# Routing the first sequence during layer A's last chunks, with tile pools split into groups

## The chip, the cores and the metric

The kernel runs on one core of one Trainium2 chip. The metric is the device time of one execution in microseconds (us). The time before is the median of three runs.

## What is computed

The reference works on two sequences of 1024 tokens with 512 features, in float32. Four layers follow one another, each a residual on a normalised input:

```python
x = x + attn_a(layernorm(x))      # layer A: Mamba2 chunked scan, 64 heads of 16, chunks of 128 tokens
x = x + ffn(layernorm(x))         # mixture of 8 experts, 2 per token, and shared experts
x = x + attn_b(layernorm(x))      # attention among the 16 heads of each token
x = x + ffn(layernorm(x))         # the same mixture again

def attn_a(u):
    xBCzA = u @ in_proj_w.T                       # x, B, C | z | A_log
    xBC = silu(causal_conv4(xBC))
    dt = softplus(A_log)
    # per chunk and head: Y_diag = (C B^T * exp(segsum(-dt))) X, Y_off from the carried state
    return ((y_ssm + D * x / dt) * silu(z + z_bias)) @ out_proj_w.T

def ffn(x):
    gates = softmax(x @ router_w.T)               # 8 experts
    masked = top2(gates) / (sum + 1e-20)
    routed = sum_e (silu(x @ wg[e]) * (x @ wu[e])) @ wd[e] * masked[:, e]
    return routed + (silu(x @ sg) * (x @ su)) @ sd      # the shared experts, 2 x 352 wide
```

`attn_b` has low-rank projections (Wc, Wcq, Wqr, Wckv, Wck, Wkr, Wv, Wo), a rotary part, and attention among the 16 heads of each token. It is not touched by the change; only the loads of its weights matter here.

## The kernel before

The residual `x` stays in SBUF as 16 tiles `xs` of 128 tokens, eight for each sequence. Line numbers are those of the kernel before.

**Layer A (L176 to L545)** works on 16 chunks of 128 tokens, two to a segment, first those of one sequence, then those of the other. For a segment, `segment_inputs` (L200) makes the projections on TensorE (`ps_ch` L285, `ps_z` L310), the convolution on VectorE (`chan` L288 to L292) and softplus, and writes the running sums of dt to DRAM (`sums`). For a chunk, `prologue` (L341) makes the chunk's x and B tiles, the carried state and `y`; `scores` (L421) makes `g`; `own` (L435) does the heads. `own` handles eight lots of eight heads, in two halves `e`. For each lot a tile `m` (128 x 8 x 128) is filled by a broadcasting DMA from `sums` (L449, on SyncE's queue, SP), then GpSimd subtracts (L453), ScalarE takes Relu and Exp (L455, L456), VectorE multiplies by `g` (L457), and TensorE adds 16 products to `ps_y` (L461). After a half, VectorE makes `yT` (L480); after both, `ps_out` (L487) is the projection back, and VectorE adds it to `x` (L495). The tag `m` has a ring of 8 buffers. The main loop calls `own` for one chunk after another as a generator; `due` and `rate` say after which of its steps a step of the next segment's inputs is taken, so that TensorE has both kinds of work in its queue. The order of instructions on each engine is the order in which these generators issue them, moved a little by a scheduler; each engine works through its own queue in order.

**The mixture (L586 to L873)** is a class `Mixture`, one object for each sequence and layer. `normalise(t)` (L709) has three steps for a tile of 128 tokens: normalise it and store its rows (`normed`, L712); transpose it (`ps_xnT`, L169; copied by ScalarE to `p_xnT`, L170) and store it (`columns`, L716); make the router's logits (`ps_p` L720, `parts` L722 on ScalarE, `ps_l` L724, `logits` L725). `route` (L586) has four steps and turns the logits of a sequence into a list of 23 blocks of 128 token slots: `r_e` (L617) marks the chosen experts, `ps_n` (L622 to L626) counts them, `ps_t` (L687) inverts the list, `r_tok` holds the tokens and `r_expi` the expert of each block. `units(lead)` (L766) is the main work: 16 shared units (two groups of shared experts by eight tiles) and 23 routed ones (the blocks), in an order that begins with `lead` shared units. Shared units read columns `xT` (L763) and weights `s_gu` and `s_d` (L742, on SP); routed ones read the block's expert number into a register on SP (L748), load that expert's `w_gu` and `w_d` (L742) and gather the tokens' rows `xg` with an indirect DMA of GpSimd (L753). A unit is `ps_g` (L816), Silu (L818), `ps_u` (L825), the product `h` (L826), three transposes `ps_hT` (L837), copies `hT` (L839, L840) and `ps_o` (L847). `after` (L856) gathers the routed results and adds them.

**The border between the two.** Layer A's pools (`a_w`, `a_seg`, `a_chunk`, `a_ps`) are closed after its last chunk, and the pools behind (`b_w`, `b_ffn`, `b_attn`, `b_ps`) are opened in the same memory: a tile of these waits for what lay there before. Just after the pools are opened, `w_router`, the attention's weights and biases are loaded in 18 DMAs from ScalarE's queue (L559, L567, L582). `w_router` and `quarters` serve `normalise`. Then the stages follow, where `run` (L1014) issues a step of its other arguments beside each step of the first, by a rate:

```python
first = [Mixture(b) for b in range(NB)]
for _ in each(first[0]):                     # all eight tiles of normalise, nothing beside them
    pass
run(first[0].units(5), 1.0, first[0].route(), each(first[1]), first[1].route())
second = [Mixture(b) for b in range(NB)]
run(first[1].units(0), 1.3, first[0].after(False), attention(0, second[0]))
run(second[0].units(6), 1.3, in_turn(first[1].after(False), second[0].route()), attention(1, second[1]))
run(second[1].units(6), 2.0, in_turn(second[0].after(True), second[1].route()))
```

Of the kernel before, what the change touches and what calls it, by code (L numbers as in the profile page):

```python
# [73 lines left out]

@with_exitstack
def hybrid_layer_kernel(ctx: ExitStack, tc: tile.TileContext, a: dict, out: bass.AP):
# [41 lines left out]
    def count(shape, pattern, base, channel_multiplier, name):  # L118

        whole = const.tile(shape, I32, name=name + "_i")  # L120
        nc.gpsimd.iota(whole, pattern=pattern, base=base, channel_multiplier=channel_multiplier)
        c = const.tile(shape, F32, name=name)
        nc.vector.tensor_copy(c, whole)
        return c

    token_of = count([P, TPB], [[P, TPB]], 0, 1, "token_of")
    place = count([P, P], [[1, P]], -P, 0, "place")
    block_of = count([P, NBLK], [[1, NBLK]], 0, 0, "block_of")
    block_at = count([P, NBLK], [[P, NBLK]], 0, 0, "block_at")
    minus_half = const.tile([P, 1], F32, name="minus_half")  # L130
# [41 lines left out]

    with ExitStack() as sa:
        wp = sa.enter_context(tc.tile_pool(name="a_w", bufs=1))  # L176
        sp = sa.enter_context(tc.tile_pool(name="a_seg", bufs=2))
        cp = sa.enter_context(tc.tile_pool(name="a_chunk", bufs=2))
        pp = sa.enter_context(tc.tile_pool(name="a_ps", bufs=2, space=PSUM))
# [20 lines left out]
        def segment_inputs(b, s, before):  # L200
# [32 lines left out]
            sv = sp.tile([P, n], F32, tag="sp_s", name="sp_s", bufs=1)  # L233
# [3 lines left out]
            acc = sp.tile([P, n], F32, tag="sp_acc", name="sp_acc", bufs=1)  # L237
# [197 lines left out]
        def own(c, gs, between):  # L435
# [8 lines left out]
            for e in range(2):  # L444
                ps = pp.tile([P, 4, P], F32, tag="y", name="ps_y", bufs=1)
                for i in range(4):
                    h0 = (2 * i + e) * 8
                    m = cp.tile([P, 8, P], F32, tag="m", name="m", bufs=8)
# [59 lines left out]

        for _ in inputs(0):
            pass  # L510
# [23 lines left out]
        for c in range(CHUNKS):  # L534
            steps = own(c, gs, before_chunk(c + 1))
            while True:
                try:
                    next(steps)
                except StopIteration as end:
                    gs = end.value  # L540
                    break
                due += rate
                while due >= 1.0:
                    due -= 1.0
                    next(side, None)  # L545

# [4 lines left out]
    fp = ctx.enter_context(tc.tile_pool(name="b_ffn", bufs=2))  # L551
    ap = ctx.enter_context(tc.tile_pool(name="b_attn", bufs=2))
    pp = ctx.enter_context(tc.tile_pool(name="b_ps", bufs=2, space=PSUM))
    dram = ctx.enter_context(tc.tile_pool(name="b_dram", bufs=4, space=bass.MemoryType.DRAM))


    w_router = wp.tile([P, KD, 32], F32, name="w_router")
    nc.vector.memset(w_router, 0.0)
    nc.scalar.dma_start(out=w_router[:, :, 0:NE], in_=a["routerT"].rearrange("(k p) e -> p k e", p=P))  # L559
    quarters = wp.tile([P, NE], F32, name="quarters")  # L560
    nc.vector.tensor_copy(quarters, ident[:, 0:NE])
    for k in range(1, KD):
        nc.vector.tensor_add(quarters, quarters, ident[:, 32 * k : 32 * k + NE])
# [21 lines left out]

    def route(logits):  # L586

        s3 = [P, TPB, NE]
        mx = fp.tile([P, TPB], F32, tag="r_mx", name="r_mx", bufs=1)
        nc.vector.tensor_reduce(mx, logits, AX.X, ALU.max)
        gt = fp.tile(s3, F32, tag="r_g", name="r_g", bufs=1)
        nc.vector.tensor_tensor(gt, logits, bc(mx, 2, NE), ALU.subtract)
        nc.scalar.activation(gt, gt, AF.Exp)
        sm = fp.tile([P, TPB], F32, tag="r_sm", name="r_sm", bufs=1)
        nc.vector.tensor_reduce(sm, gt, AX.X, ALU.add)
        nc.vector.reciprocal(sm, sm)  # L600
        nc.vector.tensor_tensor(gt, gt, bc(sm, 2, NE), ALU.mult)
        mine, other = bc(gt, 3, NE), bc(gt, 2, NE)
        n = TOPK * TPB
        ahead = fp.tile([P, TPB, NE, NE], F32, tag="r_room", name="r_ahead")
        more = fp.tile([P, TPB, NE, NE], F32, tag="r_room", name="r_more")
        nc.vector.tensor_tensor(ahead, other, mine, ALU.is_equal)
        nc.vector.tensor_tensor(ahead, ahead, bc(earlier, 1, TPB), ALU.mult)
        nc.vector.tensor_tensor(more, other, mine, ALU.is_gt)
        nc.vector.tensor_add(ahead, ahead, more)
        rank = fp.tile(s3, F32, tag="r_k", name="r_k", bufs=1)  # L610
        nc.vector.tensor_reduce(rank, ahead, AX.X, ALU.add)

        chosen = fp.tile([P, TOPK] + s3[1:], F32, tag="r_c", name="r_c", bufs=1)
        for c in range(TOPK):
            nc.vector.tensor_scalar(chosen[:, c], rank, float(c), None, ALU.is_equal)
        either = fp.tile(s3, F32, tag="r_e", name="r_e", bufs=1)
        nc.vector.tensor_add(either, chosen[:, 0], chosen[:, 1])  # L617
        yield


        ps_n = pp.tile([P, TPB + 1, NE], F32, tag="at", name="ps_n")
        nc.tensor.matmul(ps_n[:, 0:TPB], upper, either, start=True, stop=False)  # L622
        for t in range(1, TPB):
            nc.tensor.matmul(ps_n[:, t:TPB], ones, either[:, 0 : TPB - t], start=False, stop=(t == TPB - 1))
        for t in range(TPB):
            nc.tensor.matmul(ps_n[:, TPB], ones, either[:, t], start=(t == 0), stop=(t == TPB - 1))  # L626

        nc.vector.tensor_mul(gt, gt, either)
        nc.vector.tensor_reduce(sm, gt, AX.X, ALU.add)
        nc.vector.tensor_scalar(sm, sm, GATE_EPS, None, ALU.add)  # L630
        nc.vector.reciprocal(sm, sm)
        nc.vector.tensor_tensor(gt, gt, bc(sm, 2, NE), ALU.mult)
        picked = fp.tile([P, TOPK] + s3[1:], F32, tag="r_p", name="r_p", bufs=1)
        gates = fp.tile([P, TOPK, TPB], F32, tag="r_gates", name="r_gates")
        for c in range(TOPK):
            nc.vector.tensor_mul(picked[:, c], chosen[:, c], gt)
        nc.vector.tensor_reduce(gates, picked, AX.X, ALU.add)

        yield


        full = fp.tile([P, NE, TPB], F32, tag="r_e", name="r_full", bufs=1)
        nc.vector.tensor_tensor(full, bc(ps_n[:, TPB], 2, TPB), bc(block_at[:, 0:TPB], 1, NE), ALU.is_gt)
        blocks = fp.tile([P, NE], F32, tag="r_blocks", name="r_blocks", bufs=1)
        nc.vector.tensor_reduce(blocks, full, AX.X, ALU.add)
        before = fp.tile([P, NE, NE], F32, tag="r_k", name="r_before", bufs=1)
        nc.vector.tensor_tensor(before, earlier, bc(blocks, 1, NE), ALU.mult)
        first = fp.tile([P, NE], F32, tag="r_first", name="r_first", bufs=1)
        nc.vector.tensor_reduce(first, before, AX.X, ALU.add)
        past = fp.tile([P, NBLK, NE - 1], F32, tag="r_room", name="r_past")  # L650
        nc.vector.tensor_tensor(past, bc(block_of, 2, NE - 1), bc(first[:, 1:NE], 1, NBLK), ALU.is_ge)
        experts = fp.tile([P, NBLK], F32, tag="r_exp", name="r_exp", bufs=1)
        nc.vector.tensor_reduce(experts, past, AX.X, ALU.add)
        experts_i = fp.tile([P, NBLK], I32, tag="r_expi", name="r_expi")
        nc.vector.tensor_copy(experts_i, experts)


        nc.vector.tensor_scalar(first, first, float(P), -1.0, ALU.mult, ALU.add)
        number = fp.tile(s3, F32, tag="r_num", name="r_num", bufs=1)
        nc.vector.tensor_tensor(number, ps_n[:, 0:TPB], bc(first, 1, TPB), ALU.add)  # L660
        for c in range(TOPK):
            nc.vector.tensor_mul(picked[:, c], chosen[:, c], number)
        slot = fp.tile([P, TOPK, TPB], F32, tag="r_slot", name="r_slot", bufs=1)
        nc.vector.tensor_reduce(slot, picked, AX.X, ALU.add)
        slots = fp.tile([P, TOPK, TPB], I32, tag="r_slots", name="r_slots")
        nc.vector.tensor_copy(slots, slot)
        yield


        flat = slot.rearrange("p c t -> p (c t)")  # L670
        reached = fp.tile([P, n, NBLK], F32, tag="r_room", name="r_reached")
        nc.vector.tensor_tensor(reached, bc(flat, 2, NBLK), bc(block_at, 1, n), ALU.is_ge)
        block = fp.tile([P, n], F32, tag="r_blk", name="r_blk", bufs=1)
        nc.vector.tensor_reduce(block, reached, AX.X, ALU.add)
        offset = fp.tile([P, n], F32, tag="r_off", name="r_off", bufs=1)
        nc.vector.scalar_tensor_tensor(offset, block, float(-P), flat, ALU.mult, ALU.add)
        nc.vector.tensor_scalar(block, block, -1.0, None, ALU.add)
        nc.vector.tensor_tensor(reached, bc(block_of, 1, n), bc(block, 2, NBLK), ALU.is_equal)
        for c in range(TOPK):
# [12 lines left out]
        yield  # L692
        return gates, slots, tokens, experts_i

    class Mixture:

# [394 lines left out]
```

## Time and profile before

| what | value |
|---|---|
| median of 3 runs | 2448.04 us (2441.32 to 2453.75) |
| the profiled execution, its own time | 2449.53 us |
| its span in the profile | 2447.3 us, 29948 instructions |
| mean granted clock of TensorE | 0.964 |
| TensorE (PE) busy | 2254.1 us |
| VectorE (DVE) busy | 1401.5 us |
| GpSimd (POOL) busy | 1101.6 us |
| ScalarE (ACT) busy | 856.1 us |
| layer A | to 780.0 us, the end of its last `ps_out` |
| first mixture stage (`first[0].units`) | to 1161.85 us |

How the profile is read: one execution was recorded, and times are us from the start of its span. PE is TensorE's matmuls and PEld its weight loads, which lie beside them. "ACTq" and "SPq" are the issues of DMAs on the queues of ScalarE and SyncE; they are not counted as busy time of the engine. In a timeline a row has start, duration, engine, line, operation, and the tile written and those read, and behind them in brackets the idle time of that engine just before, with what ended it. PEclk is the clock that TensorE was granted, as a share of full speed.

### The profile page before, as it was taken

Reading aid. Unit: us, or ns where it says so; the run is one execution under the profiler, and the core shown is the slowest. Engines: PE = TensorE matmul, PEld = TensorE weight load, DVE = VectorE, ACT = ScalarE, POOL = GpSimd, SP = SyncE. Lnnn points to the kernel's source line nnn. Section 1 sums busy time; section 2 is a strip of 40 time slices with the busy share of each in tenths; the row PEclk is TensorE's granted clock in tenths of the full one; section 3 lists DMA queues with packets and bytes.
Section 4 is the critical chain, followed back from the end, with each engine's and each line's share of the span. In section 5 each row is a group of like instructions: output and inputs, shape, how many; then the busy total and the mean of one; then the engine's idle time right before and its main releaser. Section 6 shows DMA issues by size and latency. Waiting matters only on the chain.

```text
span 2447.3 us, 29948 instructions
## 1 busy us (share of the span) xinstructions
PE 2254.1 (92%) x10996; PEld 1450.8 (59%) x10996; DVE 1401.5 (57%) x2113; ACT 856.1 (35%) x1412; POOL 1101.6 (45%) x757
## 2 busy tenths in 40 slices
PE   7989999999996899999789899999988999899997
PEld 6766676676673556655555555556555555566564
DVE  6867777767764421002159888883688999620002
ACT  4665665666473331211122222221222323112221
POOL 3444553554463110002287777732878885210002
PEclk9999999999998899999899999999999999999998
DMA  8445454444444477775634454343555554468774
GB/s 278 150 137 169 136 172 157 157 164 148 154 167 153 160 250 248 297 263 202 220 128 162 168 191 161 135 144 108 212 186 188 182 186 149 159 252 298 263 267 139
DMA packets 119313, 456.42 MB, mean 187 GB/s; under 512 B 17280, under 2 KB 20096, under 8 KB 106368
## 3 DMA queue, kind: packets, MB, share of 16 engines
q1 hardware_dynamic: 86416, 384.87, 45.2%
q0 software_dynamic: 12480, 40.90, 5.5%
q10 hardware_dynamic: 20272, 28.74, 3.2%
q8 instruction: 88, 1.44, 0.2%
q14 instruction: 57, 0.47, 0.1%
HBM read 408.84 MB, written 45.61 MB: 186 GB/s over the span
## 4 chain that ended last, share of the span: by engine, by line
PE 59%; DVE 14%; POOL 9%; DMA 8%; ACT 6%; issue 4%; ACTq 0%; SPq 0%; POOLq 0%; DVEq 0%
PE ps_o L847 12%; PE ps_u L825 11%; PE ps_g L816 10%; PE ps_ch L285 6%; POOL pr L940 5%; PE ps_out L487 4%; DMA part<-made,r_slots 4%; DVE sc L941 3%; PE ps_z L310 3%; PE ps_xnT L169 2%; DMA m<-sums 2%; PE ps_y L461 2%; DVE o L958 2%; DVE pv L957 2%; PE ps_hT L837 2%
## 5 line engine op out<-in xcount | busy, mean ns | idle before, releaser
L940 POOL TENSOR_TENSOR pr<-qk 128x1536 f32<-128x1536 f32 x128 | 441.2, 3458 | 96.7 <-DVE sc L941 83.1
L453 POOL TENSOR_TENSOR m<-m,cum 128x1024 f32<-128x1024 f32 x128 | 241.7, 1897 | 338.6 <-DMA m<-sums 170.5
L826 DVE TENSOR_TENSOR h<-h,ps_u 128x352 f32<-128x352 f32 x156 | 80.5, 516 | 461.6 <-PE ps_u L825 457.4
L753 POOL DMA_INDIRECT xg<-normed,r_tok x92 | 90.2, 981 | 509.7 <-PE ps_xnT L169 438.2
L285 PE MATMUL ps_ch<-xnT,w_ch 128*128 128x259 f32 x1024 | 259.3, 402 | 15.6 <-DVE chan L292 14.8
L847 PE MATMUL ps_o<-w_d,hT 128*128 128x512 f32 x552 | 260.1, 603 | 0.2
L941 DVE TENSOR_REDUCE sc<-pr 128x32 f32<-128x1536 f32 x128 | 224.5, 1754 | 52.3 <-POOL pr L940 50.8
L818 ACT ACTIVATE h<-ps_g 128x352 f32<-128x352 f32 x156 | 72.3, 464 | 511.8 <-PE ps_g L816 505.3
L825 PE MATMUL ps_u<-w_gu,xT 128*128 128x352 f32 x736 | 242.0, 468 | 0.0
L816 PE MATMUL ps_g<-w_gu,xT 128*128 128x352 f32 x736 | 240.2, 465 | 0.9 <-DMA w_gu<-in_wall 0.8
L285 PEld LDWEIGHTS ps_ch<-xnT,w_ch 128*128 128x128 f32 x1024 | 194.2, 196 | 63.8 <-issue 32.6
L455 ACT ACTIVATE m<-m 128x1024 f32<-128x1024 f32 x128 | 134.2, 1053 | 195.1 <-POOL m L453 194.7
L847 PE MATMUL ps_o<-s_d,hT 128*128 128x512 f32 (+1 forms) x384 | 188.3, 621 | 8.2 <-ACT hT L839 6.2
L816 PEld LDWEIGHTS ps_g<-w_gu,xT 128*128 128x128 f32 x736 | 138.8, 192 | 95.6 <-issue 39.3
L853 ACT COPY y<-ps_o 128x512 f32<-128x512 f32 x92 | 53.9, 586 | 361.9 <-PE ps_o L847 361.9
L292 DVE SCALAR_TENSOR_TENSOR chan<-ps_ch,convw,chan 128x256 f32<-128x256 f32 x384 | 176.0, 476 | 4.7
L816 PE MATMUL ps_g<-s_gu,xT 128*128 128x352 f32 x512 | 171.3, 472 | 3.3 <-ACT h L818 1.9
L825 PEld LDWEIGHTS ps_u<-w_gu,xT 128*128 128x128 f32 x736 | 135.8, 195 | 64.4 <-issue 11.3
L825 PE MATMUL ps_u<-s_gu,xT 128*128 128x352 f32 x512 | 169.6, 467 | 0.0
L847 PEld LDWEIGHTS ps_o<-w_d,hT 128*128 128x128 f32 x552 | 105.2, 194 | 103.3 <-issue 85.6
L957 DVE TENSOR_TENSOR pv<-sc,vT 128x1024 f32<-128x1024 f32 x128 | 155.9, 1218 | 0.8
L958 DVE TENSOR_REDUCE o<-pv 128x64 f32<-128x1024 f32 x128 | 155.1, 1211 | 1.0
(209 smaller groups left out, 3532.0 us busy)
## 6 DMA issues: line engine op xcount, KB each, us to landing
w_gu<-in_wall SPq DMA_DIRECT2D x92, 1408.0 KB, 7.8
w_d<-in_wall SPq DMA_DIRECT2D x92, 768.0 KB, 4.6
m<-sums SPq DMA_DIRECT2D x128, 512.0 KB, 4.6
w_ch<-in_wch SPq DMA_DIRECT2D x96, 512.0 KB, 4.1
made<-y ACTq DMA_DIRECT2D x92, 256.0 KB, 6.6
xT<-columns SPq DMA_DIRECT2D x64, 256.0 KB, 4.8
s_gu<-in_wall SPq DMA_DIRECT2D x8, 1408.0 KB, 7.0
normed<-xn SPq DMA_DIRECT2D x32, 256.0 KB, 2.0
```

Of the source, the lines that this page charges most:

```text
L285: nc.tensor.matmul(ps, w[:, ct % 2, k], xnT[:, k, :], start=(k == 0), stop=(k == KD - 1))
L292: nc.vector.scalar_tensor_tensor(c[:, i], ps[:, tap : tap + SEG], convw[:, ct, tap : tap + 1], c[:, i], ALU.mult, ALU.add)
L453: nc.gpsimd.tensor_tensor(m, m, bc(cum[:, j, h0 : h0 + 8], 2, P), ALU.subtract)
L455: nc.scalar.activation(m, m, AF.Relu)
L487: nc.tensor.matmul(ps_out, yT[:, e, i, :], w_out[:, 2 * i + e, :], start=(e == 0 and i == 0), stop=(e == 1 and i == 3),)
L816: nc.tensor.matmul(ps_g, xT[:, k, :], both[:, k, 0, :], start=(k == 0), stop=(k == KD - 1))
L825: nc.tensor.matmul(ps_u, xT[:, k, :], both[:, k, 1, :], start=(k == 0), stop=(k == KD - 1))
L847: nc.tensor.matmul(ps_o, hT[:hn, c, :], wd[:hn, c, :], start=(c == 0), stop=(c == len(HC) - 1))
L940: nc.gpsimd.tensor_mul(pr, bc(qks[t][:, 0, i : i + IC, :], 2, AH), bc(qks[t][:, 1], 1, IC))
L941: nc.vector.tensor_reduce(scores[t][:, i : i + IC, :], pr, AX.X, ALU.add)
L957: nc.vector.tensor_tensor(pv, bc(scores[t][:, i : i + IC, :], 2, DH), bc(vs[t], 1, IC), ALU.mult)
L958: nc.vector.tensor_reduce(outs[t][:, i : i + IC, :], pv, AX.X, ALU.add)
```

## The change

- `route` and `Mixture` are defined ahead of layer A, with pools of their own (`mix`, `mix_dram`), which live to the end. `w_router` and `quarters` are made at the kernel's start. Their small PSUM tiles come from a helper `small`, in layer A under the tag `misc`, which `ps_out` uses too, later under `at`.
- The eight `normalise` of the first sequence and its `route` are issued as single steps during layer A's chunks of the second sequence, one step at every second step of `own`.
- `route` copies `ps_n` to a tile `counts`, and reads that.
- Four pools are split into groups (class `Pools`): `a_seg` in three, `a_ps` in four, `b_ffn` in four and `b_ps` in six, so that the memory of each comes free by itself. The integer tables of the start have a pool that is closed early. In softplus two tiles take the memory of others (`sv = y`, `acc = r`).
- The ring of `m` has 6 buffers, not 8.
- The first stage begins with 4 shared units, not 5, has no `normalise` and no `route` of its own sequence beside it, and loads `s_gu` and `s_d` of its first group from ScalarE's queue.

```diff
+class Pools:
+    def __init__(self, ctx, tc, name, groups, **kw):
+        self.pool_of = {}
+        for i, tags in enumerate(groups):
+            pool = ctx.enter_context(tc.tile_pool(name=f"{name}{i}", bufs=2, **kw))
+            self.pool_of.update((tag, pool) for tag in tags)
+    def tile(self, shape, dtype, tag, **kw):
+        return self.pool_of[tag].tile(shape, dtype, tag=tag, **kw)
...
+    mp = ctx.enter_context(tc.tile_pool(name="mix", bufs=2))
+    mdram = ctx.enter_context(tc.tile_pool(name="mix_dram", bufs=4, space=bass.MemoryType.DRAM))
+    small_tag = "misc"
+    def small(shape, name):
+        return pp.tile(shape, F32, tag=small_tag, name=name, bufs=2)
...
-        sp = sa.enter_context(tc.tile_pool(name="a_seg", bufs=2))
+        sp = Pools(sa, tc, "a_seg", [
+                ["xnT", "w_ch", "al", "sp_y", "sp_r", "sp_s2", "row"],
+                ["dt", "dw", "decay", "chan"],
+                ["cum", "gate0", "gate1"]])
-        pp = sa.enter_context(tc.tile_pool(name="a_ps", bufs=2, space=PSUM))
+        pp = Pools(sa, tc, "a_ps", [["y"], ["g0", "g1"], ["misc"], ["proj"]], space=PSUM)
...
-            sv = sp.tile([P, n], F32, tag="sp_s", name="sp_s", bufs=1)
+            sv = y
...
-            acc = sp.tile([P, n], F32, tag="sp_acc", name="sp_acc", bufs=1)
+            acc = r
...
-                    m = cp.tile([P, 8, P], F32, tag="m", name="m", bufs=8)
+                    m = cp.tile([P, 8, P], F32, tag="m", name="m", bufs=6)
...
+        first = [Mixture(b) for b in range(NB)]
+        routes = chain(*(first[0].normalise(t) for t in range(TPB)), first[0].route())
+        turn = 0
...
                 while due >= 1.0:
                     due -= 1.0
                     next(side, None)
+                if c >= TPB:
+                    turn += 1
+                    if turn % 2 == 0:
+                        next(routes, None)
+        for _ in routes:
+            pass
...
-    fp = ctx.enter_context(tc.tile_pool(name="b_ffn", bufs=2))
+    fp = Pools(ctx, tc, "b_ffn", [["s_gu", "s_d"], ["xT", "h", "hT"], ["w_gu"], ["w_d", "xg", "y", "part"]])
-    pp = ctx.enter_context(tc.tile_pool(name="b_ps", bufs=2, space=PSUM))
+    pp = Pools(ctx, tc, "b_ps", [["sc"], ["at"], ["o"], ["tr"], ["g"], ["u"]], space=PSUM)
+    small_tag = "at"
...
+        counts = mp.tile([P, TPB + 1, NE], F32, tag="r_n", name="r_n", bufs=1)
+        nc.vector.tensor_copy(counts, ps_n)
...
-        def weights(self, row):
+        def weights(self, row, queue=None):
...
-                nc.sync.dma_start(out=w, in_=src)
+                (queue or nc.sync).dma_start(out=w, in_=src)
...
-        def units(self, lead):
+        def units(self, lead, queue=None):
...
-            shared = {0: self.weights(NE)}
+            shared = {0: self.weights(NE, queue)}
...
-    first = [Mixture(b) for b in range(NB)]
-    for _ in each(first[0]):
-        pass
-    run(first[0].units(5), 1.0, first[0].route(), each(first[1]), first[1].route())
+    run(first[0].units(4, nc.scalar), 1.0, each(first[1]), first[1].route())
```

## The prediction

> **What bounds the kernel now.** I read the page first, part 1 and then its strips by slices (part 2), for the engine that is short and the places where it is not busy; then the chain of waits, the table by stage, the timeline of the worst stretch, and the instruction orders of both kernels.
>
> ```profile
> PE 2254.1 (92%) x10996; PEld 1450.8 (59%) x10996; DVE 1401.5 (57%) x2113; ACT 856.1 (35%) x1412; POOL 1101.6 (45%) x757
> PE   7989999999996899999789899999988999899997
> PEclk9999999999998899999899999999999999999998
> ```
>
> TensorE (PE) is busy 92% of the span, so a change pays by filling a hole. The hole is in slices 12 and 13 (one is 61.2 us): PE reads 6 and 8, the clock 8 and 8. That is the border between layer A (the chunks) and the mixtures. The table by stage (start and end, length, PE, PEld, VectorE, ScalarE and GpSimd busy, clock, DMA share, GB/s) cuts it out:
>
> ```profile
> 380.00:740.00 360.00, 344.64 (x2588) 249.72 (x2590) 259.83 (x441) 227.54 (x254) 184.59 (x119) 0.98 0.49 159
> 740.00:780.00 40.00, 30.84 (x336) 20.21 (x324) 18.42 (x20) 18.71 (x20) 19.23 (x11) 0.91 0.30 106
> 780.00:806.84 26.84, 5.04 (x33) 3.50 (x34) 3.34 (x12) 3.23 (x6) 2.11 (x6) 0.60 0.88 295
> 806.84:880.00 73.16, 69.57 (x358) 43.41 (x356) 26.88 (x81) 26.38 (x54) 16.08 (x35) 0.91 0.51 177
> 880.00:1162.00 282.00, 276.75 (x1023) 166.61 (x1021) 44.68 (x104) 61.60 (x157) 35.71 (x41) 0.98 0.71 252
> ```
>
> In the third row, from the last `ps_out` to the first unit's `ps_g`, PE is busy 5.04 of 26.84 us. The timeline (start, duration, engine) says why:
>
> ```profile
> 780.03 0.41 ACTq L567 DMA_DIRECT2D w_c<-in_Wc  x1
> ...
> 782.59 4.13 ACTq L567 DMA_DIRECT2D w_cq<-in_Wcq  x1
> ...
> 797.38 0.59 ACTq L567 DMA_DIRECT2D sin<-in_sin  x1
> 798.07 0.59 ACT L170 COPY p_xnT<-ps_xnT 128x512 f32<-128x512 f32 x1 [31.63 <-DMA b_rows<-in_brope]
> 798.71 0.65 PE L720 MATMUL ps_p<-p_xnT,w_router 128*32 128x128 f32 x8 [17.27 <-ACT p_xnT L170]
> ```
>
> Eighteen loads, w_router's and seventeen of attention weights, are issued from ScalarE's queue, and ScalarE computes nothing from 780.0 to 798.07. The copy that turns the first normalised tile stands behind them, and PE waits 17.27 us for it. The rest of the stretch is the serial `normalise` of the first sequence.
>
> **Why the parts move as they do.** In the new order the seventeen loads still stand after the last `ps_out` (`w_c` waits for PE, since the b_w tiles lie over layer A's memory). New is what lies around them. Ahead of the last `ps_out` stand `ps_g` and `ps_u` of unit 0, `ps_g` of unit 1 and half its `ps_u`, and one tile's transposes; behind it, before PE needs ScalarE again: the rest of `ps_u`, two `ps_hT`, `ps_g` and `ps_u` of unit 2, one `ps_p`. Then PE meets `ps_l`, which needs ScalarE's `parts` copy, and that is behind the loads.
>
> **Before, from 806.84 on.** The chain gives a steady unit as `ps_g` 2.37, `ps_hT` 0.33, transposes of a gathered tile 0.44, `ps_u` 2.37, `ps_o` 2.58 us: 8.09 routed, 7.65 shared. The 23 routed and 16 shared units make 308.5. Beside them run the rest of the first sequence's normalise (5.3), its route (0.17 + 1.52 + 1.79 and four lots of `ps_t`, 6.8), the second's normalise (8 × 0.97 = 7.8) and route (6.9): 335.3 in all. Losses: PE at half clock after idle times 1.3 + 1.7 + 2.7 + 1.7 = 7.4; the first gather, behind the late route, 3.6; the stage's last wait and the clock after it 5.1 + 2.6. 806.84 + 335.3 + 18.7 = 1160.8; the trace has 1161.85.
>
> **After, from the last `ps_out`.** Let E be what layer A becomes longer, so that `ps_out` ends at 780.0 + E. ScalarE is blocked for 18.0 and then copies `parts` (0.3): 798.3 + E. PE's ready work behind `ps_out` is 1.2 + 2 × 0.33 + 2 × 2.37 + 0.36 = 6.9, so it still idles 11.4. Units done by then: 3 × 2.37 + 1.2 ahead of `ps_out`, 6.6 behind: 14.9. PE work left: 308.5 − 14.9 + 7.8 − 0.85 (already made) + 6.9 = 307.5. Losses left: 1.3 + 1.7 of clock and 7.7 at the end; the gather's wait goes, since the route is ready some chunks earlier. Sum: 798.3 + 307.5 + 10.7 = 1116.5 + E, against 1160.8: 44.3 − E.
>
> The 18.0 is the unsure term. Freed by the same `ps_out`, w_d of block 0 and w_gu and w_d of block 1 (0.77 + 1.41 + 0.77 MB) now go out on SP while the 4.2 MB of the seventeen do. Before, s_gu and s_d (about 2.1 MB) did that, and they now load earlier: nearly the same load, so I keep 18.0. Least: seventeen issues at the 0.45 us of the short rows, 8. Most: all 7.2 MB at the stretch's 336 GB/s, 21.4. The row that bears on it: from 780 to 798 the DMA engines are 97% busy at 336 GB/s while two queues issue.
>
> The Trainium skill speaks against moving transfers between issuers: "DMA: Bandwidth & Descriptors", section "Issuing engines are not separate DMA queues", says that transfers of all issuers share the same 16 engines, so that another queue saves only the issuing engine's time. The 97% agrees. By the rule the block would take the 21.4 rather than the 18.0, and the gain would be 3.4 less.
>
> **What E costs.** Layer A takes in 8 × 0.97 + 6.8 = 14.6 us of PE work. From 380 to 740 PE has 15.4 us idle, in waits of 0.3 to 3.3 us for the conv's DVE work and ScalarE; the added matmuls wait for DVE and ScalarE too, so I take a third, 5, as filled. Then two waits. The nearest rows for route's lumps on DVE are PE's 4.4 us for `r_e` (L617), once, and for a tile's `xn` 33.8 us in 15 times, 2.3 each. With `y`, `m` and chunk work between the steps I take one 4.4 and no `xn`. DVE gets about 21 us more in some 300 (72% to near 79% busy), ScalarE 13; neither becomes the bound.
>
> The m ring goes from eight buffers to six. SP's loads already wait for their buffers 219.6 us in 99 times, and POOL waits 170.5 us for m's DMA, yet PE hardly waits for m between 380 and 740. By the rows of chunk 14, its seventh and eighth m come 4 to 5 us later with six; elsewhere there are 5 to 17 us to spare. I take 2.4. At the last chunk the delay of about 5 is covered, because `yT` now stands ahead of the last m products on DVE, which removes this:
>
> ```profile
> 768.53 3.50 PE L461 MATMUL ps_y<-m,xc 128*32 128x128 f32 x64 [6.44 <-DVE yT L480]
> ```
>
> So E = 14.6 − 5 + 2.4 + 4.4 = 16.4. Lower bound 0 (all added work fits the idle time). Upper bound 45: 14.6, eight times 2.3 for `xn`, the whole 8.2 of the `parts` waits, 4.4.
>
> **Edits at about nothing.** The router's weights, `quarters` and the index tables' pool move to the kernel's start: one load's issue (0.52) and 0.85 us of DVE (0.17 + 0.11 + 0.57), in a start where DVE is busy 20 of 30 us; nothing, at most 1.4. The four extra copies of `ps_n` (0.2 us each, like DVE's other 128x64 rows) hide under PE's 92%; uncovered, 0.8. Twenty-three reads of expert numbers on SP now stand in chunk 13, the largest lot ahead of m loads: by the 0.26 and 0.15 us of SP's rows about 7 us in that lot, hidden by the m loads' spare time; at worst those 7. Unit 0's three xT and block 0's w_gu stand on SP ahead of the last two m loads: 7.8 us of transfer shared with them, under the same `yT`. Silu and Exp alternate once or twice on ScalarE near the end. Lead 5 to 4 permutes units. The softplus buffers' sharing adds waits only inside one serial DVE chain. The later stages keep their order (3147 of about 3395 PE instructions stand in the same sequence) and are taken as unchanged.
>
> **Sum.** 44.3 − 16.4 = 27.9. The profiled execution took 2449.53 us (span 2447.3), 1.5 above the median 2448.04; 2449.5 − 27.9 = 2421.6 there, 2420 as a median. This kernel's measurement can tell about 0.5% (12.2 us) from no change.
>
> **The rivals.**
> - The loads block ScalarE for only 8 us: PE's 6.9 cover most, and both the idle and the half clock go. That adds 10 to 12: about 2409. For it: s_gu and s_d are out of the way, and `w_cq`'s 4.13 looks like waiting for room in the queue. Against: three other large loads take their place at the same moment. Chance 0.12.
> - Layer A pays in full: E of 32 to 40 from `xn` and `parts` waits (or the early units do not fit ahead of `ps_out`, 10 less). 44.3 − 32 = 12, 44.3 − 40 = 4: 2436 to 2444, within 0.5%. For it: every step crosses PE, ScalarE and DVE between queued chunk work. Against: a step only every second turn, with other PE work between. Chance 0.14. The change not doing what it says would show here too.
> - Slower: the ring of six. Were m late by 4 us in each of the 16 chunks, E would be 16.4 − 2.4 + 64 = 78 and the time 34 longer, 2482. It decides from E = 44.3 + 12.2 = 56, 2.6 us per chunk. For it: the 99 waits of SP for m's buffers. Against: PE's waits from 380 to 740 name the conv, not m. Chance 0.12.
>
> My forecast has 0.62; its own range, from E and the block, is 2405 to 2435. Leaving out the slow rival and the lowest part of the first, the range is 2402 to 2446. Faster takes 0.62 + 0.12 and a little of the second rival, 0.75; same 0.13; slower 0.12.
>
> **What would show it.** Right: after the last `ps_out` PE still idles about 11 us, ended by ScalarE's `parts` behind the loads; the first routed unit waits for no gather; first `ps_g` before the last `ps_out`; `ps_out` of chunk 15 at 790 to 800; the mixture stage ends near 1133. Wrong: waits of PE for m (L457's successor) or for `xn` in many chunks; the last `ps_out` beyond 825; a block after it under 10 or over 22 us; or the later stages moving by more than 10 us.

## The result, and the profile after

| | before | after |
|---|---|---|
| median of 12 runs | 2448.12 us | 2452.4 us (2447.14 to 2455.9) |
| ratio | | 1.0016, 95% interval 1.0000 to 1.0031 |
| span of the profiled execution, clock | 2447.3 us, 0.964 | 2454.1 us, 0.964 |
| last `ps_out` of layer A ends | 780.0 us | 823.6 us |
| last `ps_o` of the first mixture stage ends | 1175.4 us | 1176.1 us |

Nothing was gained: the time is the same within 0.5%, where 2420 (2402 to 2446) was forecast. (The 1161.85 us given above for the stage leaves out its very last product, which stands behind a wait; here it is counted in all kernels.) Behind this stage the order is the same, and the remaining 1271.9 us before and 1278.0 after lie within what this part took in the other runs below (1266.7 to 1281.7).

So the first stage did gain its time: from the last `ps_out` to its end it takes 42.9 us less. But layer A became 43.6 us longer. The strips of the page after, by slices of 61.4 us:

```profile
PE   7999999999898799998889899999988999899997
PEclk9999999999979899999899999999999999999998
```

The hole of before (6 and 8 in slices 12 and 13, counted from 0) has become an 8 and a 7, and the clock now falls to 7 in slice 11, inside layer A. The table by stage for chunk 12 (from the previous chunk's last `ps_out` to its own; columns as before), first of before, then of after:

```profile
663.10:707.10 44.00, 43.71 (x328) 31.60 (x327) 31.50 (x53) 31.25 (x34) 23.44 (x14) 1.00 0.55 180
```
```profile
674.00:742.50 68.50, 63.21 (x388) 48.36 (x388) 48.84 (x97) 31.44 (x34) 25.20 (x17) 0.80 0.32 108
```

In this chunk the route's steps lie. It takes 24.5 us more, and PE is *busy* 19.5 more, for 6.8 us of added matmuls: the clock is 0.80, so the same work takes longer. After the last `ps_out` the forecast's picture is there (first the row of the table by stage, then the timeline, both of after):

```profile
823.60:847.08 23.48, 7.16 (x35) 4.39 (x35) 1.90 (x3) 0.32 (x2) 3.14 (x3) 0.70 0.95 339
```
```profile
846.12 0.59 ACTq L902 DMA_DIRECT2D sin<-in_sin  x1
846.76 0.27 ACT L343 COPY parts<-ps_p 128x128 f32<-128x128 f32 x1 [25.84 <-DMA b_rows<-in_brope]
847.08 0.59 PE L345 MATMUL ps_l<-quarters,parts 128*128 128x8 f32 x2 [16.32 <-ACT parts L343]
```

PE does its 7.16 us of ready work and then idles for 16.32, until `parts` is made behind the loads.

Where layer A grew is read from the ends of each chunk's last `ps_out` (us against the kernel before, out of the traces; e1 and e2 are explained below):

| end of chunk | 8 | 9 | 10 | 11 | 12 | 13 | 14 | 15 |
|---|---|---|---|---|---|---|---|---|
| after | -2.4 | 4.3 | 3.3 | 10.9 | 35.4 | 36.1 | 45.1 | 43.6 |
| e1, route not in the chunks | 0.6 | 6.8 | 5.9 | 13.7 | 15.2 | 15.2 | 22.8 | 17.3 |
| e2, no routing in the chunks | -0.2 | -1.1 | -2.2 | -2.2 | -2.3 | -1.7 | 4.1 | -1.1 |

Each row is one execution. Chunks 0 to 7 hold no step of the routing, and yet chunk 7 ends between 8.1 us earlier and 1.5 later than in the kernel before, according to the run. A firmer measure is the time from the end of chunk 7 to that of chunk 13: 265.2 us before, 304.9 after (304.3 in e4, whose chunks are the same), 281.3 in e1 (281.0 in its repeat e11) and 263.2 in e2.

### The profile page after: what moved, and what is told of

Read it like the earlier page. It is cut to its first block, busy times and chain, and to the rows that moved or that the text cites. A ratio compares the mean times of both kernels' runs of the same rounds, so it can differ in the third digit from the quotient of the medians.

```text
span 2454.1 us, 29957 instructions
## 1 busy us (share of the span) xinstructions
PE 2261.6 (92%) x10996; PEld 1456.7 (59%) x10996; DVE 1413.0 (58%) x2117; ACT 859.1 (35%) x1414; POOL 1101.5 (45%) x757
## 4 chain that ended last, share of the span: by engine, by line
PE 58%; DVE 16%; POOL 10%; DMA 8%; ACT 5%; issue 4%; ACTq 0%; POOLq 0%; DVEq 0%
PE ps_o L468 11%; PE ps_u L446 11%; PE ps_g L437 10%; PE ps_ch L617 6%; POOL pr L988 4%; PE ps_out L819 4%; DVE sc L989 3%; DMA part<-made,r_slots 3%; PE ps_z L642 3%; DMA m<-sums 3%; PE ps_xnT L185 2%; DVE o L1006 2%; PE ps_y L793 2%; DVE pv L1005 2%; POOL m L785 2%
## 5 line engine op out<-in xcount | busy, mean ns | idle before, releaser
L617 PE MATMUL ps_ch<-xnT,w_ch 128*128 128x259 f32 x1024 | 259.3, 399 | 18.0 <-DVE chan L624 17.1
L789 DVE TENSOR_TENSOR m<-m,g 128x1024 f32<-128x1024 f32 x128 | 151.0, 1213 | 34.9 <-ACT m L788 34.4
```

Source lines behind the costliest of these rows:

```text
L617: nc.tensor.matmul(ps, w[:, ct % 2, k], xnT[:, k, :], start=(k == 0), stop=(k == KD - 1))
L789: nc.vector.tensor_tensor(m, m, bc(gs[e][:, i, :], 1, 8), ALU.mult)
```

## The experiments

The theory after the result (theory 1) is that route's four steps are what is dear among the chunks. Its rivals are the ring of six, the normalise steps and the pools.

**e1: route behind layer A, normalise still in the chunks.**

```diff
-        routes = chain(*(first[0].normalise(t) for t in range(TPB)), first[0].route())
+        routes = chain(*(first[0].normalise(t) for t in range(TPB)))
...
-    run(first[0].units(4, nc.scalar), 1.0, each(first[1]), first[1].route())
+    run(first[0].units(5, nc.scalar), 1.0, first[0].route(), each(first[1]), first[1].route())
```

> The eight normalise steps stay in layer A's chunks, the four steps of route go back beside the first stage's lead units (5 of them, as in the kernel before). Theory 1 (route's steps are dear among the chunks: its DVE operations are held up to about 2 us each while GpSimd subtracts, PE waits for them, and its narrow matmuls run at half clock): chunk 12 falls from 68.5 to about 46 us, the last ps_out ends near 800 instead of 823.6, route then costs about 14 us beside the units, in all near 2443. Rival (the ring of six or the normalise steps make layer A longer): the last ps_out stays at 815 or later and the time is 2460.

Measured: 2429.8 us, 0.9918 of the kernel before (0.9896 to 0.9941); the last `ps_out` at 797.3. Chunk 12 by the table by stage, and the 20.7 us behind the last `ps_out`:

```profile
676.80:722.30 45.50, 42.09 (x323) 30.16 (x323) 39.46 (x71) 28.53 (x32) 26.36 (x17) 1.00 0.49 163
797.30:818.00 20.70, 16.35 (x91) 13.24 (x90) 9.98 (x29) 0.48 (x2) 0.31 (x1) 0.83 0.96 340
```

Chunk 12 is back to 45.5 us at full clock. Theory 1 holds, but the time is 13 us better than the 2443 it said. The second row and the timeline of PE tell why:

```profile
797.14 1.35 PE L446 MATMUL ps_u<-s_gu,xT 128*128 128x352 f32 x4
798.32 0.33 PE L241 MATMUL ps_n<-r_e,upper 128*128 128x64 f32 x2
798.49 1.68 PE L243 MATMUL ps_n<-r_e,ones 128*128 128x56 f32 x14
800.02 1.93 PE L245 MATMUL ps_n<-r_e,ones 128*128 128x8 f32 x16
801.81 2.61 PE L437 MATMUL ps_g<-s_gu,xT 128*128 128x352 f32 x8
...
808.15 1.07 PE L308 MATMUL ps_t<-r_reached,r_at 128*128 128x23 f32 x8 [1.03 <-DVE r_reached L302]
```

ScalarE is blocked by the loads here too (busy 0.48 of 20.7 us), but PE is busy 16.35: route's `ps_n` and `ps_t` need VectorE and not ScalarE, and stand in the stretch where after has its 16.32 us of idle PE. From the last `ps_out` to the stage's end e1 needs 357.0 us and after 352.5: route costs 4.5 there (7.5 by the repeat e11, with 360.0). Among the chunks it cost 20.9 (36.1 against 15.2 at the end of chunk 13), or 23.6 counted from the end of chunk 7.

**e2: no routing in the chunks** (pools split, ring of six, loads of `s_gu` and `s_d` as in the change; 5 lead units).

```diff
-        routes = chain(*(first[0].normalise(t) for t in range(TPB)), first[0].route())
+        routes = iter(())
...
-    run(first[0].units(4, nc.scalar), 1.0, each(first[1]), first[1].route())
+    for _ in each(first[0]):
+        pass
+    run(first[0].units(5, nc.scalar), 1.0, first[0].route(), each(first[1]), first[1].route())
```

> Everything of the change but the early routing: normalise and route stand again after layer A, as in the kernel before; pools split, ring of six, s_gu and s_d from ScalarE's queue, 5 lead units. Theory 1: layer A grows only by the units' matmuls placed ahead of its end and by the ring, the last ps_out ends near 785 to 790, in all 2440 to 2450. Rival (the ring of six or the pools make layer A longer): the last ps_out ends at 805 or later, in all above 2465.

Measured: 2444.33 us, 0.9986 (0.9973 to 0.9999); last `ps_out` at 778.9, earlier than theory 1's 785 to 790, the total as it said. The pools and the ring do not make layer A longer. By the table above the normalise steps then cost 17 us (e1 15.2 against e2's -1.7 at chunk 13), or 18 counted from the end of chunk 7. Over chunks 8 to 11 PE is busy 10.2 us more and idle 6.9 more. These are rows of what it waits for there (total, times, longest), first in e1, then in e2:

```profile
PE ps_ch L617 <- DVE chan L624: 6.8, 2, 3.8
PE ps_y L793 <- DVE yT L812: 4.9, 2, 2.9
...
PE ps_x L687 <- ACT p_xnT L186: 1.2, 2, 0.8
PE ps_l L345 <- ACT parts L343: 1.0, 2, 0.8
```
```profile
PE ps_ch L617 <- DVE chan L624: 4.9, 2, 3.2
```

The steps' own waits (`p_xnT`, `parts`) are 2.2 us. More comes from the chunks' own VectorE work (`chan`, `yT`), for which PE waits 11.7 us in e1 and 4.9 in e2; in e11 it is 11.8.

**e3: the ring of six, in the kernel before.**

```diff
-                    m = cp.tile([P, 8, P], F32, tag="m", name="m", bufs=8)
+                    m = cp.tile([P, 8, P], F32, tag="m", name="m", bufs=6)
```

> The kernel before with the ring of m at 6 buffers and nothing else. Theory 1 (the ring bears only on chunks 14 and 15, where the m of a chunk are needed every 3 us): last ps_out 2 to 8 us later, in all 2450 to 2456. Rival (the ring lengthens all chunks): over 20 us more, 2468 or above.

Measured: 2451.06 us, 1.0001 (0.9981 to 1.0022). The ring costs nothing that the total shows, and the rival falls. It does cost something in chunk 14, which takes 23.9 us instead of 16.9: PE idles there for 4.9 us, where it idled for none. These are the two largest of its waits:

```profile
PE ps_out L487 <- DVE yT L480: 2.8, 1, 2.8
PE ps_y L461 <- DVE m L457: 1.6, 2, 1.2
```

Chunk 15 is shorter in turn, so that the two together take 3.1 us more. (The last `ps_out` still ends 2.1 us earlier than before, at 777.9 and not 2 to 8 later, because chunks 0 to 7 took 4.8 less in this execution.)

**e4: the seventeen loads from GpSimd's queue**, in the changed kernel.

```diff
-        nc.scalar.dma_start(out=w, in_=src)
+        nc.gpsimd.dma_start(out=w, in_=src)
...
-        nc.scalar.dma_start(out=b_rows[:, i, :], in_=a[name].partition_broadcast(P))
+        nc.gpsimd.dma_start(out=b_rows[:, i, :], in_=a[name].partition_broadcast(P))
```

> The changed kernel with the seventeen attention loads issued from GpSimd's queue instead of ScalarE's. Theory 1 (after the last ps_out PE waits 16.3 us only because ScalarE stands at those issues): the idle time and most of the 17 us of half clock behind it go, in all about 2432. Rival (the transfers themselves are in the way, whoever issues them): PE waits for weights instead, gain under 5 us.

Measured: 2447.46 us, 0.9983 (0.9958 to 1.0008). From the last `ps_out` to the stage's end it takes 349.9 us against after's 352.5: 2.6 gained, not 20. In the total it is not told apart from after, as the intervals overlap. The timeline:

```profile
839.12 0.58 ACT L186 COPY p_xnT<-ps_xnT 128x512 f32<-128x512 f32 x1 [4.46 <-DMA columns<-p_xnT]
839.73 0.32 SPq L337 DMA_DIRECT2D columns<-p_xnT  x1
839.76 0.43 PE L341 MATMUL ps_p<-p_xnT,w_router 128*32 128x128 f32 x8 [4.28 <-ACT p_xnT L186]
```

ScalarE is free, but its copy into the one `p_xnT` buffer waits until the store of the previous one has landed, and that store is among the loads' transfers (last issue at 852.5): it took 7.5 us from issue to landing, where the one ahead of the loads took 2.1. PE waits 4.28 us here and 4.06 once more. The theory fell, and the rival is right that the transfers are in the way whoever issues them, though PE waits for `p_xnT` and not for weights. The shorter waits gain little for a second reason. Over the whole stage PE idles 8.0 us less than in after (21.3 against 29.3) but is busy 5.4 more. Both have 27.3 us of half clock; in after 17.1 of them lie over PE's long wait and just behind it, in e4 more of them fall where PE works.

The Trainium skill ("DMA: Bandwidth & Descriptors", section "Issuing engines are not separate DMA queues") says that another issuer saves only the time to issue. The 2.6 us gained agree with that.

**e5, e6, e7: e1 with the normalise steps at every third step of the chunks, with the loads on GpSimd's queue, and with both.**

```diff
-                    if turn % 2 == 0:
+                    if turn % 3 == 0:
```

> As e1 (route after layer A), and the normalise steps at every third step of the chunks instead of every second, so that they spread over about seven chunks and not five. Theory 1 (each step pays by its own waits and by half clock where several meet): chunks 9 and 11 lose less, the last ps_out ends some 4 to 6 us earlier than e1's 797.3, in all near 2425. Rival (what normalise costs is its own PE work and the ring of six in chunk 14, whatever the pace): no change within 2 us of e1's 2430.

> e1 (route after layer A) with the seventeen attention loads issued from GpSimd's queue. Theory 1 (in e1 route's PE and DVE work stands over ScalarE's 20 us at the loads, so the block is already covered): within 4 us of e1. Rival (the loads still hold back the units in e1): 8 us or more below e1, near 2420.

> e5 and e6 together. Theory 1: e5's time within 4 us, 2421 to 2427. Rival: below 2418.

Measured: 2436.9 us, 0.9931 (0.9900 to 0.9962), then 2430.25, 0.9892 (0.9846 to 0.9937), and 2433.99, 0.9915 (0.9884 to 0.9946). None is told apart from e1. Theory 1 missed e5 (2425) and e7 (2421 to 2427): the slower pace gains nothing (e5's last `ps_out` 798.4 against 797.3; theory 1 had 4 to 6 earlier), so nothing speaks for crowding as the cause of the normalise cost. That e6 gains nothing fits the reading that route covers the stretch in which ScalarE is blocked.

**e8: a probe of the clock and of VectorE beside GpSimd.**

```python
for n, times in ((512, 40), (8, 200), (512, 30), (23, 160), (512, 30), (64, 120), (512, 30), (128, 100), (512, 30)):
    for i in range(times):
        nc.tensor.matmul(ps[:, 0:n], turns[i % 4], xs[0][:, 0:n], start=True, stop=True)
```

> A kernel that computes nothing of the layer: it copies x to the output, and beside that TensorE runs streams of matmuls without a pause, with 512, 8, 512, 23, 512, 64, 512, 128 and 512 columns, and VectorE runs short operations (128x8 and 128x512 from SBUF, 128x256 with a source in PSUM) once alone and once while GpSimd subtracts 128x1024. Theory 1: the narrow streams (8 and 23 columns) are granted half clock though PE never waits, 512 stays at full clock; the SBUF operations of VectorE last up to about 2 us more when they meet a GpSimd subtract, the PSUM ones do not. Rival: the clock stays full in the narrow streams (then the half clock in chunk 12 came from PE's waits alone); VectorE's times do not change (then the long ones in the trace have another cause).

Stretches inside the streams of 8, 512, 23, 512 and 64 columns:

```profile
45.00:125.00 80.00, 80.00 (x372) 79.48 (x373) 13.40 (x25) 6.32 (x4) 0.50 0.00 1
130.00:150.00 20.00, 20.00 (x48) 8.93 (x47) 0.00 (x0) 0.00 (x0) 1.00 0.00 0
160.00:218.00 58.00, 58.00 (x268) 57.32 (x269) 0.00 (x0) 0.00 (x0) 0.50 0.00 1
225.00:240.00 15.00, 15.00 (x36) 6.65 (x35) 0.00 (x0) 0.00 (x0) 1.00 0.00 0
250.00:270.00 20.00, 20.00 (x182) 20.00 (x181) 0.00 (x0) 0.00 (x0) 1.00 0.01 2
```

PE is busy all the time, yet the streams of 8 and 23 columns run at a clock of 0.50, from 2.4 and 3.8 us after their start to some 4 us behind their end, and each matmul (two records of the profile) takes 0.427 us. The stream of 64 columns keeps 1.00 and 0.223 us each, as does that of 128. A change of the stationary operand for every matmul is in all of them.

The same probe shows VectorE beside GpSimd's subtracts. The 128x8 operations from SBUF take 0.16 us alone and 1.46 to 1.67 beside them:

```profile
3.78 0.16 DVE L174 TENSOR_SCALAR thin<-thin 128x8 f32<-128x8 f32 x1
19.70 1.46 DVE L174 TENSOR_SCALAR thin<-thin 128x8 f32<-128x8 f32 x1
```

Those with a source in PSUM take 0.47 in both cases. The 128x512 products stay at 0.68, as each began just as a subtract had ended; those subtracts then take 2.3 us, not 1.9. In after's chunk 12 the same is seen:

```profile
715.74 1.89 POOL L785 TENSOR_TENSOR m<-m,cum 128x1024 f32<-128x1024 f32 x1 [3.42 <-DMA m<-sums]
716.04 1.63 DVE L298 TENSOR_SCALAR r_blk<-r_blk 128x16 f32<-128x16 f32 x1
...
718.88 1.89 POOL L785 TENSOR_TENSOR m<-m,cum 128x1024 f32<-128x1024 f32 x1 [1.25 <-DMA m<-sums]
719.03 2.21 DVE L302 TENSOR_TENSOR r_reached<-r_reached,token_of 128x184 f32<-128x184 f32 x2
721.04 0.41 PE L308 MATMUL ps_t<-r_reached,r_at 128*128 128x23 f32 x1 [2.95 <-DVE r_reached L302]
```

`r_blk` took 0.17 us before, where GpSimd was idle, and 1.63 here: it ends just after the subtract. All of route on VectorE takes 24.6 us instead of 15.5. Not every operation from SBUF is held, though. In the same chunk a reduction and a reciprocal of route ran at their usual length inside a pair of subtracts:

```profile
679.63 3.80 POOL L785 TENSOR_TENSOR m<-m,cum 128x1024 f32<-128x1024 f32 x2
680.10 0.21 DVE L218 TENSOR_REDUCE r_sm<-r_g 128x8 f32<-128x64 f32 x1
680.62 0.19 DVE L219 RECIPROCAL r_sm<-r_sm 128x8 f32<-128x8 f32 x1
```

**e9: route's narrow matmuls widened to 64 columns**, in the changed kernel.

```diff
-            nc.tensor.matmul(ps_n[:, t:TPB], ones, either[:, 0 : TPB - t], ...)
+            nc.tensor.matmul(ps_n[:, TPB + t : 2 * TPB + t], ones, either, ...)
...
-            nc.tensor.matmul(ps_n[:, TPB], ones, either[:, t], ...)
+            nc.tensor.matmul(ps_n[:, 0:TPB], ones, padded_e[:, t : t + TPB], ...)
...
-                    ps_t, at[:, i], reached[:, i0 + i], ...
+                    ps_t, at[:, i], room[:, (i0 + i) * NBLK : (i0 + i) * NBLK + 64], ...
```

> The changed kernel with route's narrow matmuls widened to 64 columns (zeros or unused columns beside the wanted ones; ps_n gets 16 matmuls of 64 columns for 16 of 8 to 64, ps_t 16 of 64 for 16 of 23; three small memsets more on VectorE), the routing at its place in the chunks. By the probe a 64-column matmul costs the 0.22 us of a narrow one and keeps the full clock. Theory 1 (the narrow matmuls held the clock at half for 27.3 us of chunk 12): the half clock in chunk 12 falls to about 7 us, the chunk from 68.5 to about 58, the last ps_out ends near 813, in all near 2441. Rival (the waits for VectorE set the clock and the time): half clock and time as before the edit, 2452.

Measured: 2447.61 us, 1.0001 (0.9977 to 1.0025). Chunk 12:

```profile
677.10:737.90 60.80, 54.49 (x387) 40.78 (x388) 50.80 (x100) 28.75 (x32) 25.61 (x17) 0.92 0.36 122
```

Half clock falls from 27.3 us of the chunk to 10.2, the chunk from 68.5 to 60.8: 7.7 gained with more columns multiplied, where theory 1 had 10.5. In the total the gain is not told apart from none, as the intervals of e9 and after overlap; theory 1's 2441 and its last `ps_out` near 813 were missed (821.0).

**e10 and e11: the widening on top of e1, and e1 again on the same chip.**

> e1 (route after layer A) with the same widening in all four routes. Theory 1: the 10 us of half clock behind the last ps_out and some near the other routes go, 4 to 8 us below e1. Rival: as e1 within 2 us.

> e1 once more on the chip of e9 and e10, for the comparison with e10: 0.992 of the kernel before.

Measured: e10 2427.74 us, 0.9918 (0.9899 to 0.9936), e11 0.9940 (0.9919 to 0.9961). Whether the widening helps once route stands behind layer A is open: 0.2% lies between them, with overlapping intervals. e1 and e10 beat both the kernel before and the changed one.

## Why the prediction failed, point by point

- **The gain at the border held.** 44.3 us were forecast and 42.9 measured (43.6 of E, less the 0.7 by which the stage ends later). Inside it the block, the stretch in which the loads hold ScalarE, was mis-sized: from the first issue to the ScalarE copy behind the loads it was 23.1 us (823.7 to 846.76), not 18.0, at a DMA share of 0.95 and 339 GB/s, and PE idled 16.3, not 11.4. The estimate of 21.4, all 7.2 MB at 336 GB/s, was a better guide than the length of before's block. That w_d and w_gu of the first blocks shared the transfers is the likely cause; it was not tried alone. Something else in the stage was about 3.5 us better; that was not itemised.
- **The step that failed is "What E costs".** E was put at 16.4 and is 43.6, near the upper bound of 45, but the bound's terms were other ones. Of the 34 us between the 2421.6 forecast for the profiled execution and its 2455.9, E makes 27 and the later stages 6, which is within their 15 us of difference between runs. By e1 and e2 E splits into 17 for normalise, 20.9 for route, 7.5 in chunks 14 and 15, and -1.7 for the pools. Counted from the end of chunk 7 it is 47: 18 for normalise, 23.6 for route, 7.5 in chunks 14 and 15, and -2.0 for the pools.
- *Route*: 6.8 of matmuls and 4.4 for one wait were counted. What the runs showed is the clock: 27.3 us of chunk 12 ran at half, which costs 13.7 of PE's time; e9 cut that to 5.1 by widening alone, and the chunk by 7.7. Durations of narrow matmuls had been taken from rows of the first mixture stage, where units with 352 columns stand between them. The other part is waits for VectorE (1.8 and 2.9), behind operations held by GpSimd; "one `r_e` wait" was the right size but the wrong place. The two go together: each of the chunk's two half-clock stretches (10.2 us from 689.8 and 17.1 from 720.5) begins in or just after one of these waits, with the narrow matmuls behind it. With wide ones (e9) PE still waits, 2.3 us at the longest, and the stretches last 6.8 and 3.4.
- *Normalise*: 7.8 of matmuls, of which 5 (with route's) were to fill idle time. PE's idle time did not fall, but rose by 6.9 over chunks 8 to 11, in waits for `yT` and `chan` above all. A wait was looked for in the moved steps, and it came in the chunk's own steps. That the moved steps push back the VectorE work of these is the likely reason; it was not tried alone.
- *Units ahead of the last `ps_out`*: counted as finished work at no cost, as they were to fill the 9.2 us of idle PE in chunk 15. Chunks 14 and 15 grew by 7.5. Chunk 14 has 5.5 us of new idle time, 3.0 of them for `yT` and 1.5 for m, and this comes from the ring of six: e3, with the ring alone, has the same waits (2.8 and 1.6). The ring so takes 3.1 of the 7.5, near the 2.4 forecast. It also leaves only 4.5 us of idle time in chunk 15 (e3), so the 9.0 us of units there fill it and do not all fit; the other 4.4 are left to them. E has no term for the units, and lets the `yT` wait that goes cover the ring's delay, so the same idle time was used twice.
- **Right:** the ring (e3), and the gather's wait, 3.1 us before and gone after. No cost shows for the copies of `ps_n` and for the reads of expert numbers on SP (chunk 13, where these stand, takes 0.7 us more); neither they nor the lead of 4 were tried alone.
- **The rivals.** The second, layer A pays in full, is what happened; its E of 32 to 40 was even passed, and so its 2436 to 2444 was too low. But its waits were not the ones: from chunk 8 on PE waits 0.7 us for `parts` and never for `xn` in layer A, and it knew nothing of the clock. The short block of the first is refuted (23.1 us), the ring's 4 us a chunk by e3.
- **What the change missed:** it put route at a place where it costs 21 to 24 us, while behind the last `ps_out` it costs 4.5 to 7.5. The 16 us hole there was the place for it.

## What to carry to other kernels

Work that is moved into a busy stage is paid at that stage's clock and with its waits for other engines, not with the durations it had where it stood: look what runs on the neighbouring engines there. A stretch where one engine is blocked is the right home for steps that do not need this engine; here route behind layer A, beside ScalarE's blocked 20 us, made the kernel 0.6 to 0.8% faster than before (e1 and e11). Narrow matmuls may be worth widening with unused columns, since 64 columns took no longer than 8 in the probe; here it shortened chunk 12 (e9), and whether it shortens the total is open. Where two changes use the same idle time, it counts once.

## What was not expected of the hardware

- A stream of float32 matmuls with 8 or 23 columns is granted half the clock although PE never pauses (0.427 us each); with 64 columns the clock stays at 1.00 and each takes 0.223 us. The Trainium skill ("TensorE: Matmul & The Clock Gate", section "Part 1: The HAM clock gate") says that the gate goes by how busy PE has been in windows of about 3.4 us. The runs agree with the length of the windows (half-clock stretches of 3.4, 6.8, 10.2 and 17.1 us), but in the probe a stream of narrow matmuls that the profile shows as busy without a pause did not keep the full clock.
- An elementwise VectorE operation with its operands in SBUF that meets a GpSimd subtract of 128x1024 waits for its end: 0.16 us becomes 1.46 to 1.67 in the probe. Operations with a source in PSUM stay at 0.47, and in chunk 12 a reduction (0.21) and a reciprocal (0.19) from SBUF were not held either. The skill ("Trainium Architecture — The Big Picture", section "What this means for kernel authors") calls the port pair that the two engines share an exclusive lock; the probe agrees for the operations that are held.
